# A hybrid convolution, attention and recurrence layer on one core: softmax with a maximum pass for every group and the recurrence in 64 runs per image, in place of softmax without the pass and one recurrence over all images

## The chip, the cores and the metric

The kernel runs on one core of one Trainium2 chip. The metric is the device time of one execution in microseconds (us). Before the change the median of three runs is 23558.29 us (23557.13 to 23570.37). Engines are named as in the profile: PE (matmul) and PEld (its weight loads), DVE (vector), ACT (scalar), POOL, and SP, whose queue issues the DMAs.

## The reference

Everything is float32. The input x has 32 images of 128 channels and 64 x 64 = 4096 places. Layer 0 adds a convolution with a kernel of its own for every image. Layer 1 takes the places as tokens and adds windowed attention (16 wide, 4 heads of 4, windows of 144 tokens at a stride of 72), then a recurrence over the 4096 tokens of each image:

```python
x = x + _L0_conv_ref(_gn(x), L0_conv_kernels, L0_conv_fc_w, L0_conv_fc_b)
t = _to_tokens(x)
t = t + _L1_attn_ref(_ln_t(t),
...
)
t = t + _L1_ffn_ref(_ln_t(t), L1_ffn_W, L1_ffn_V, L1_ffn_gamma, L1_ffn_beta)
x = _from_tokens(t, x)
```

The two parts that the change touches are the softmax of the attention and the recurrence:

```python
scores = jnp.einsum('nhqd,nhkd->nhqk', q, k) / np.float32(np.sqrt(HD))
attn = jax.nn.softmax(scores, axis=-1)
...
Wx = jnp.einsum('bti,hi->bth', x, W)
mean = jnp.mean(flat, axis=0)
var = jnp.var(flat, axis=0)
Wx = ((flat - mean) * jax.lax.rsqrt(var + BN_EPS) * gamma + beta).reshape(B, T, H)
def step(yt, wx_t):
    yt = jax.nn.sigmoid(wx_t + yt @ Vt)
    return (yt, yt)
_, ys = jax.lax.scan(step, y0, jnp.swapaxes(Wx, 0, 1))
```

The mean and the variance run over all tokens of all images, so the recurrence can begin only when the last image has its W z. V is the orthogonal factor of a QR decomposition.

## The kernel before, in words

Line numbers are those of the profile. Channels lie on the 128 partitions, the places of an image along the free dimension, in blocks of 512.

*Stage one, the images* (`images`, L240). A loop over 32 images (L592) calls `front` of the next image, then `attention` and `tail` of the current one. A scheduler orders the instructions of each engine by their dependencies, pools of buffers limit how far it runs ahead. `front` (L295) loads x, normalises it by groups, mixes the convolution kernel (L343 to L346), runs the convolution as nine products per block (L354), and normalises by token: `norm` (L272) with products at L278 and L282, `spread` (L290) that lays the token's factor over all channels. `attention` (L411) projects to 16 (L419), transposes (L431), and works in eight groups of seven windows (the last of six). A group has q and k by L450, v by L470, and then for each window and each pair of heads a set of four score products (L496), one exponential over the set (L504), and four products with v (L510). A column of ones in v gives the sum of each row, by which L529 and L531 divide between two rounds of transposes (L525, L536). L552 leads back to 128 channels. The tiles `sc` for scores have two buffers in PSUM.

`tail` (L568) normalises again, adds to x, stores the sum x2 (L575), normalises once more to z, multiplies a block by W only for its mean and variance (L585, L586), and stores z (L587), both in chunks of 128 places, so that the second stage reads them as [chunk, channel, image, place].

*The branch.* L195 to L236 work out a bound on the scores from the weights and load it to a register. At L599 the kernel takes `images(False)` where the bound is small enough, otherwise `images(True)`, which differs by `shift` (L374): it forms the scores a first time with q and k exchanged (L383), takes each row's largest by DVE (L390), transposes the negated maxima (L401), and adds them to a fifth row of q, whose partner in k is one (L409).

*Stage two, the recurrence* (L605 to L667). From the mean and variance come a scale and a shift; the scale is folded into W (L621 to L625). For each of 4096 places one product with V over 32 images (L661) adds to W z, which L638 wrote into PSUM for 16 places at a time, and one sigmoid (L665) writes y. Per 128 places DVE adds y to x2 (L666) and the sum is stored (L667). Loads of the next chunk run ahead (L629).

Of the kernel before, what the change touches and what calls it, by code (L numbers as in the profile page):

```python
# [10 lines left out]
ALU = mybir.AluOpType  # L11
# [18 lines left out]
SUB = 16  # L30


@with_exitstack
def hybrid_kernel(
# [34 lines left out]
    x2_d = dram.tile([NCH, P, NB, CH], F32, name="x2_d")  # L69
    z_d = dram.tile([NCH, P, NB, CH], F32, name="z_d")  # L70
# [122 lines left out]


    bdr = const.tile([P, DK], F32, name="bdr")  # L195
    nc.sync.dma_start(bdr, b_down.partition_broadcast(P))
    ipr = const.tile([P, 3 * DK], F32, name="ipr")
    nc.sync.dma_start(ipr, in_proj_b.partition_broadcast(P))
    ipT = const.tile([DK, 3 * DK], F32, name="ipT")
    nc.sync.dma_start(ipT, in_projT)  # L200
    okf = const.tile([P, 1], F32, name="okf")
    oki = const.tile([P, 1], mybir.dt.int32, name="oki")
    with tc.tile_pool(name="sb1", bufs=1) as sb1, tc.tile_pool(
        name="ps1", bufs=1, space=bass.MemoryType.PSUM
    ) as ps1:
        one_ = sb1.tile([P, P], F32, name="one_")
        nc.vector.memset(one_, 1.0)
        w2 = sb1.tile([P, DK], F32, name="w2")
        nc.vector.tensor_mul(w2, wd[:, 0:DK], wd[:, 0:DK])
        n_ps = ps1.tile([P, 3 * DK], F32, name="n_ps")  # L210
        nc.tensor.matmul(n_ps[:, 0:DK], one_, w2, start=True, stop=True)
        xm = sb1.tile([P, DK], F32, name="xm")
        nc.scalar.activation(xm, n_ps[:, 0:DK], AF.Sqrt, scale=1.02 * P)
        nc.scalar.activation(bdr, bdr, AF.Abs)
        nc.vector.tensor_add(xm, xm, bdr)
        xmax = sb1.tile([P, 1], F32, name="xmax")
        nc.vector.tensor_reduce(xmax, xm, axis=AX.X, op=ALU.max)
        nc.scalar.activation(ipT, ipT, AF.Abs)
        nc.scalar.activation(ipr, ipr, AF.Abs)
        r_ps = ps1.tile([P, 3 * DK], F32, name="r_ps")  # L220
        nc.tensor.matmul(r_ps, one_[:DK, :], ipT, start=True, stop=True)
        qk = sb1.tile([P, 3 * DK], F32, name="qk")
        nc.vector.scalar_tensor_tensor(qk, r_ps, xmax, ipr, ALU.mult, ALU.add)
        pr_ = sb1.tile([P, NH, HD], F32, name="pr_")
        nc.vector.tensor_mul(
            pr_.rearrange("p h f -> p (h f)"), qk[:, 0:DK], qk[:, DK : 2 * DK]
        )
        sm = sb1.tile([P, NH], F32, name="sm")
        nc.vector.tensor_reduce(sm, pr_, axis=AX.X, op=ALU.add)
        smx = sb1.tile([P, 1], F32, name="smx")  # L230
        nc.vector.tensor_reduce(smx, sm, axis=AX.X, op=ALU.max)
        nc.vector.tensor_scalar(okf, smx, 60.0 / HD**-0.5, None, ALU.is_le)
        nc.vector.tensor_copy(oki, okf)

    bnst = const.tile([P, NB * NBLK, 6], F32, name="bnst")
    small = nc.values_load(oki[0:1, 0:1], min_val=0, max_val=1)  # L236
# [3 lines left out]
    def images(shifted):  # L240
        with ExitStack() as pa:
            keep = pa.enter_context(tc.tile_pool(name="keep", bufs=1))
            big = pa.enter_context(tc.tile_pool(name="big", bufs=2))
            one = pa.enter_context(tc.tile_pool(name="one", bufs=1))
            wrk = pa.enter_context(tc.tile_pool(name="wrk", bufs=2))
            sml = pa.enter_context(tc.tile_pool(name="sml", bufs=3))
            p_sc = pa.enter_context(tc.tile_pool(name="p_sc", bufs=2, space=bass.MemoryType.PSUM))
            p_mm = pa.enter_context(tc.tile_pool(name="p_mm", bufs=2, space=bass.MemoryType.PSUM))
            p_av = pa.enter_context(tc.tile_pool(name="p_av", bufs=2, space=bass.MemoryType.PSUM))

            gx = keep.tile([P, H + 2, W + 2], F32, name="gx")
            nc.gpsimd.memset(gx, 0.0)
            nr = HD + 1 if shifted else HD
            if shifted:
                mx = keep.tile([HALF, NWG, 2, P], F32, name="mx")
                nc.gpsimd.memset(mx, 0.0)
            vas = []
            for i in range(2):
                va = keep.tile([HALF, 2 * NWG, NH, 32], F32, name=f"va{i}")
                nc.gpsimd.memset(va, 1.0)  # L260
                vas.append(va)

            def mm_tile():
                return p_mm.tile([P, BLK], F32, name="mm")

            def sc_tile():
                return p_sc.tile([P, 2, BLK], F32, name="sc")

            def av_tile():
                return p_av.tile([P, BLK], F32, name="av")  # L270

            def norm(src, dst):  # L272

                var = av_tile()
                for i in range(NBLK):
                    s = slice(i * BLK, (i + 1) * BLK)
                    ps = mm_tile()
                    nc.tensor.matmul(ps, cen, src[:, s], start=True, stop=True)  # L278
                    sq = wrk.tile([P, BLK], F32, name="sq")
                    nc.scalar.activation(sq, ps, AF.Square)  # L280
                    nc.scalar.copy(dst[:, s], ps)
                    nc.tensor.matmul(  # L282
                        var, avg[:, P - i : 2 * P - i], sq, start=(i == 0), stop=(i == NBLK - 1)
                    )
                rs = wrk.tile([P, BLK], F32, name="rs")
                nc.scalar.activation(rs, var, AF.Sqrt, bias=eps)
                nc.vector.reciprocal(rs, rs)  # L287
                return rs

            def spread(rs, i):  # L290
                ps = mm_tile()
                nc.tensor.matmul(ps, row[:, i, :], rs, start=True, stop=True)  # L292
                return ps

            def front(b):  # L295
                xt = big.tile([P, T], F32, name="xt")
                for i in range(4):
                    s = slice(i * (T // 4), (i + 1) * (T // 4))
                    nc.sync.dma_start(xt[:, s], xf[b, :, s])


                st = sml.tile([P, NBLK, 6], F32, name="st")
                for i in range(NBLK):
                    nc.vector.bn_stats(st[:, i, :], xt[:, i * BLK : (i + 1) * BLK])
                mv = sml.tile([P, 2], F32, name="mv")
                nc.vector.bn_aggr(mv, st.rearrange("p i s -> p (i s)"))
                gm_ps = mm_tile()
                nc.tensor.matmul(gm_ps[:, 0:1], grp, mv[:, 0:1], start=True, stop=True)
                gm = sml.tile([P, 1], F32, name="gm")
                nc.vector.tensor_copy(gm, gm_ps[:, 0:1])  # L310
                dev = sml.tile([P, 1], F32, name="dev")
                nc.vector.tensor_sub(dev, mv[:, 0:1], gm)
                cv = sml.tile([P, 1], F32, name="cv")
                nc.vector.scalar_tensor_tensor(cv, dev, dev, mv[:, 1:2], ALU.mult, ALU.add)
                gv_ps = mm_tile()
                nc.tensor.matmul(gv_ps[:, 0:1], grp, cv, start=True, stop=True)
                gr = sml.tile([P, 1], F32, name="gr")
                nc.scalar.activation(gr, gv_ps[:, 0:1], AF.Sqrt, bias=eps)
                nc.vector.reciprocal(gr, gr)
                nc.vector.tensor_scalar(  # L320
                    gx[:, 1 : H + 1, 1 : W + 1],
                    xt.rearrange("p (h w) -> p h w", w=W),
                    gm,
                    gr,
                    ALU.subtract,
                    ALU.mult,
                )


                pl = sml.tile([P, P], F32, name="pl", bufs=1)  # L330
                nc.vector.tensor_scalar_mul(pl, dev.to_broadcast([P, P]), gr)
                lg_ps = mm_tile()
                nc.tensor.matmul(lg_ps[:, 0:NK], pl, fcwT, start=True, stop=True)
                co = sml.tile([P, NK], F32, name="co")
                nc.vector.tensor_add(co, lg_ps[:, 0:NK], fcb)
                nc.scalar.activation(co, co, AF.Tanh, scale=0.5)
                nc.scalar.activation(co, co, AF.Exp, scale=0.5)
                cs = sml.tile([P, 1], F32, name="cs")
                nc.vector.tensor_reduce(cs, co, axis=AX.X, op=ALU.add)
                nc.vector.reciprocal(cs, cs)  # L340
                nc.vector.tensor_scalar_mul(co, co, cs)
# [380 lines left out]
```

## Time and profile before

| what | value |
|---|---|
| median of three runs | 23558.29 us |
| the profiled execution | 23570.37 us |
| its span, first to last instruction | 23568.3 us |
| mean granted PE clock | 0.606 |
| PE busy | 19439.3 us (82%) |
| PEld busy | 10946.6 us (46%) |
| DVE busy | 2800.0 us (12%) |
| ACT busy | 5923.9 us (25%) |
| POOL busy | 10.7 us |

A matmul in float32 stands in the profile as two records, each with its weight load, so 14,080 score products are 28,160 records at L496. The end of a matmul's record is modelled, and records of products in different parts of the array overlap; the mean of a record is therefore longer than the pitch at which such products follow each other. The dearest groups of instructions, busy time and mean, and the idle time before them:

```profile
L510 PE MATMUL av<-ex,va 72*32 72x144 f32 x28160 | 4142.7, 448 | 1151.4 <-ACT ex L504 1151.4
L496 PE MATMUL sc<-qs,ks 4*72 4x144 f32 x28160 | 3970.3, 466 | 0.0
L661 PE MATMUL wx<-yk,fVT 128*128 128x32 f32 x8190 | 2557.4, 406 | 1449.4 <-ACT yk L665 1449.4
L504 ACT ACTIVATE ex<-sc 72x576 f32<-72x576 f32 x3520 | 2220.5, 645 | 5865.4 <-PE sc L496 5864.7
```

The first number after the bar is the time in which at least one instruction of the group was running, the second the mean length of one in ns, the third the idle time of its engine just before, with what ended it.

### The profile page before, as it was taken

The page shows a single profiled execution, that of the slowest core. Times are in us where ns is not written, and L with a number is a line of the kernel's source. Part 1 is how long each engine was busy: PE and PEld are TensorE (multiplying, and loading weights), DVE is VectorE, ACT ScalarE, POOL GpSimd, SP SyncE. Part 2 cuts the span into 40 slices and gives each one's busy share as a digit, 9 for nine tenths or more (in the row PEclk, how much of TensorE's full clock was granted, in tenths as well). Part 3 has the DMA queues.
Part 4 walks back from the last instruction along what each step waited for, and adds up shares of the span by engine and source line. Part 5 has one row for each costly group of instructions (what it writes and reads, how often), then busy time and mean ns, then how long its engine had stood idle before and what let it go on. Part 6 is the DMA issues. An engine that isn't in the chain of part 4 may idle for free.

```text
span 23568.3 us, 200944 instructions
## 1 busy us (share of the span) xinstructions
PE 19439.3 (82%) x90183; PEld 10946.6 (46%) x90183; DVE 2800.0 (12%) x3848; ACT 5923.9 (25%) x11369; POOL 10.7 (0%) x41
## 2 busy tenths in 40 slices
PE   8888888888888888888888888888888876666666
PEld 4444444444444444444444444444444444444444
DVE  1111111111111111111111111111111010000000
ACT  2222222222222222222222222222222222222222
POOL 0000000000000000000000000000000000000000
PEclk7666666666666666666666666666666555555555
DMA  0000000000000000000000000000000011111111
GB/s 12 11 11 11 11 11 11 11 11 11 11 11 11 11 11 11 11 11 11 11 11 11 11 11 11 11 11 11 11 11 11 8 43 43 47 46 47 43 47 36
DMA packets 427366, 418.25 MB, mean 18 GB/s; under 512 B 8176, under 2 KB 401792, under 8 KB 418176
## 3 DMA queue, kind: packets, MB, share of 16 engines
q1 hardware_dynamic: 426496, 405.32, 5.4%
q8 instruction: 709, 11.62, 0.2%
q14 instruction: 161, 1.32, 0.0%
HBM read 203.97 MB, written 201.33 MB: 17 GB/s over the span
## 4 chain that ended last, share of the span: by engine, by line
PE 76%; ACT 15%; DVE 6%; issue 3%; ACTq 0%; DMA 0%; SPq 0%
PE av L510 17%; PE wx L661 11%; PE sc L496 11%; PE mm L354 9%; ACT ex L504 8%; PE sc L450 6%; ACT yk L665 5%; PE mm L470 3%; PE mm L278 3%; PE mm L292 3%; PE av L282 3%; PE sc L525 2%; PE wx L638 2%; PE sc L536 2%; PE mm L552 2%
## 5 line engine op out<-in xcount | busy, mean ns | idle before, releaser
L510 PE MATMUL av<-ex,va 72*32 72x144 f32 x28160 | 4142.7, 448 | 1151.4 <-ACT ex L504 1151.4
L496 PE MATMUL sc<-qs,ks 4*72 4x144 f32 x28160 | 3970.3, 466 | 0.0
L661 PE MATMUL wx<-yk,fVT 128*128 128x32 f32 x8190 | 2557.4, 406 | 1449.4 <-ACT yk L665 1449.4
L504 ACT ACTIVATE ex<-sc 72x576 f32<-72x576 f32 x3520 | 2220.5, 645 | 5865.4 <-PE sc L496 5864.7
L510 PEld LDWEIGHTS av<-ex,va 72*32 72x32 f32 x28160 | 2027.0, 159 | 2989.1 <-ACT ex L504 2472.7
L496 PEld LDWEIGHTS sc<-qs,ks 4*72 4x72 f32 x28160 | 2535.1, 222 | 1317.6 <-issue 1281.8
L661 PEld LDWEIGHTS wx<-yk,fVT 128*128 128x128 f32 x8190 | 2086.3, 311 | 2239.3 <-ACT yk L665 2103.0
L354 PE MATMUL mm<-gx,wb 128*128 128x512 f32 x4608 | 2035.0, 604 | 214.5 <-DVE wb L345 214.5
L665 ACT ACTIVATE yk<-wx,shf 128x32 f32<-128x32 f32 x4096 | 1175.7, 287 | 3257.1 <-PE wx L661 3257.1
L354 PEld LDWEIGHTS mm<-gx,wb 128*128 128x128 f32 x4608 | 888.6, 194 | 1337.2 <-issue 1337.2
L292 PE MATMUL mm<-rs,row 128*128 128x512 f32 x1536 | 968.8, 758 | 468.2 <-DVE rs L287 436.7
L280 ACT ACTIVATE sq<-mm 128x512 f32<-128x512 f32 x768 | 464.9, 605 | 3443.2 <-PE mm L278 3443.1
L529 DVE RECIPROCAL rd<-sc 126x32 f32<-126x32 f32 (+1 forms) x256 | 91.6, 358 | 9347.1 <-PE sc L525 9347.1
L470 PEld LDWEIGHTS mm<-wv,gt 32*72 32x72 f32 x7040 | 905.3, 235 | 284.3 <-issue 170.9
L450 PE MATMUL sc<-gt,wq 32*128 32x504 f32 x1024 | 896.6, 1023 | 100.8 <-DVE gt L431 100.8
L552 PE MATMUL mm<-oc,wc 20*128 20x504 f32 (+1 forms) x1024 | 932.7, 1062 | 30.6 <-ACT oc L542 30.6
L450 PE MATMUL sc<-gt,wk 32*128 32x504 f32 x1024 | 906.9, 1037 | 0.0
L470 PE MATMUL mm<-wv,gt 32*72 32x16 f32 x7040 | 872.8, 274 | 0.0
L292 PEld LDWEIGHTS mm<-rs,row 128*128 128x128 f32 x1536 | 334.4, 236 | 1045.4 <-DVE rs L287 516.1
L282 PE MATMUL av<-sq,avg 128*128 128x512 f32 x1536 | 802.4, 641 | 0.5 <-ACT sq L280 0.5
L666 DVE TENSOR_TENSOR xk<-xk,yk 128x4096 f32<-128x4096 f32 x32 | 238.3, 7447 | 4208.8 <-ACT yk L665 4208.8
L455 ACT ACTIVATE qs<-sc,bq 128x504 f32<-128x504 f32 x512 | 531.8, 1141 | 737.0 <-PE sc L450 737.0
(133 smaller groups left out, 9371.2 us busy)
## 6 DMA issues: line engine op xcount, KB each, us to landing
xt<-in_x_dram SPq DMA_DIRECT2D x128, 512.0 KB, 5.6
x_d<-xt SPq DMA_DIRECT2D x32, 2048.0 KB, 9.3
z_d<-zt SPq DMA_DIRECT2D x32, 2048.0 KB, 9.3
zk<-z_d SPq DMA_DIRECT2D x32, 2048.0 KB, 7.6
xk<-x_d SPq DMA_DIRECT2D x32, 2048.0 KB, 7.8
out_dram<-xk SPq DMA_DIRECT2D x32, 2048.0 KB, 9.2
kT<-in_conv_k_dram SPq DMA_DIRECT2D x1, 2304.0 KB
wq<-in_in_projT_dram SPq DMA_DIRECT2D x8, 1.0 KB, 1.7
```

The source lines that it names most:

```text
L278: nc.tensor.matmul(ps, cen, src[:, s], start=True, stop=True)
L282: nc.tensor.matmul(var, avg[:, P - i : 2 * P - i], sq, start=(i == 0), stop=(i == NBLK - 1))
L292: nc.tensor.matmul(ps, row[:, i, :], rs, start=True, stop=True)
L354: nc.tensor.matmul(ps, wb[:, t, :], gx[:, 8 * i + di : 8 * i + di + 8, dj : dj + W], start=(t == 0), stop=(t == 8),)
L450: nc.tensor.matmul(ps[:, c, 0:GH], wt[rows, u, :], gf[rows, c, :], start=True, stop=True)
L470: nc.tensor.matmul(vp[:HALF, o : o + DK], gf[rows, c, HALF * m : HALF * (m + 1)], wv[rows, u, :], start=True, stop=True,)
L496: nc.tensor.matmul(ps[:HALF, j, c * WIN : (c + 1) * WIN], ks[hr : hr + nr, c, HALF * m : HALF * (m + 1)], qs[hr : hr + nr, o : o + WIN], s ...
L504: nc.scalar.activation(ex, ps[:HALF, :, 0 : 2 * WIN], AF.Exp, scale=HD**-0.5)
L510: nc.tensor.matmul(ap[32 * h : 32 * h + 32, (m - m0) * WIN : (m - m0 + 1) * WIN], va[:, 2 * m + c, h, :], ex[:, j, c * WIN : (c + 1) * WIN ...
L552: nc.tensor.matmul(ps[:, 0 : 4 * n], wc, oc[:, 4 * n * i : 4 * n * (i + 1)], start=True, stop=True,)
L661: nc.tensor.matmul(ps[:, t, :], fVT, prev, start=False, stop=True, skip_group_check=True)
L665: nc.scalar.activation(prev, ps[:, t, :], AF.Sigmoid, bias=shf)
```

## The change

The test on the weights' bound and the second copy of the image stage go; what `shift` did stands in `attention` for every group, with the fifth row of q and k always in use. In `tail`, W z is copied from PSUM over z by ACT and stored in place of z; x2 and W z are stored as one row of 4096 places per channel and image. Scale and shift are applied later, to W z. A new test takes the row sums of the absolute values of V times its transpose, and where the largest is at most 1.2 the recurrence is done by runs, otherwise by steps as before (with the scale as a diagonal matrix in the place of W).

By runs, the 4096 places of an image are 64 runs of 64. Every run begins 32 places early, from a plain sigmoid of the first of them, and its first 32 results are dropped; the first run of an image begins at zero. So one step works on the same place of 64 runs of two images, 128 columns: one product with V, one multiply-add on DVE, one sigmoid on ACT, which writes y over W z. There are 16 pairs of images, three of them in flight in three streams; after a pair POOL adds y to x2.

```diff
-    x2_d = dram.tile([NCH, P, NB, CH], F32, name="x2_d")
-    z_d = dram.tile([NCH, P, NB, CH], F32, name="z_d")
+    x2_d = dram.tile([NB, P, T], F32, name="x2_d")
+    z_d = dram.tile([NB, P, T], F32, name="z_d")
...
-        nc.vector.tensor_scalar(okf, smx, 60.0 / HD**-0.5, None, ALU.is_le)
...
+        nc.tensor.matmul(vv, fVT, fVT, start=True, stop=True)
+        nc.scalar.activation(va_, vv, AF.Abs)
+        nc.vector.tensor_reduce(vr, va_, axis=AX.X, op=ALU.add)
+        nc.tensor.transpose(vt_, vr.to_broadcast([P, P]), ident)
+        nc.vector.tensor_reduce(vm, vt_, axis=AX.X, op=ALU.max)
+        nc.vector.tensor_scalar(vm, vm, 1.2, None, ALU.is_le)
...
-                    if shifted:
-                        shift(qs, ks, nw)
+                for m in range(nw):
+                    o = m * WIN
+                    for pr in range(2):
+                        ps = sc_tile()
...
-                                            ks[hr : hr + nr, c, HALF * m : HALF * (m + 1)],
-                                            qs[hr : hr + nr, o : o + WIN],
+                                        ks[hr : hr + HD + 1, c, HALF * m : HALF * (m + 1)],
+                                        qs[hr : hr + HD + 1, o : o + WIN],
...
                 nc.vector.bn_stats(bnst[:, b * NBLK + i, :], wp)
+                nc.scalar.copy(zt[:, s], wp)
...
+            def load(g):
+                if g < NG:
+                    zs[g] = zp.tile([P, NI, NRUN, RUN], F32, name="zr")
+                    for i in range(NI):
+                        nc.sync.dma_start(
+                            zs[g][:, i].rearrange("p c r -> p (c r)"), z_d[g * NI + i]
+                        )
+            for g in range(NSTR + 1):
+                load(g)
+            def stream(j):
...
+                for g in range(j, NG, NSTR):
+                    zt = zs[g]
+                    for r in range(RUN - WARM, RUN):
+                        y, z = yw[r % 2][:, :, 1:], zt[:, :, 0 : NRUN - 1, r]
+                        if r == RUN - WARM:
+                            nc.scalar.activation(y, z, AF.Sigmoid, bias=shf, scale=scl)
+                        else:
...
+                    prev = yw[(RUN - 1) % 2]
+                    for r in range(RUN):
+                        h = hp.tile([P, NI, NRUN], F32, name=f"h{j}")
+                        ps = p_v.tile([P, NI, NRUN], F32, name=f"v{j}")
+                        nc.tensor.matmul(ps, fVT, prev, start=True, stop=True)
+                        nc.vector.scalar_tensor_tensor(
+                            h, zt[:, :, :, r], scl, ps, ALU.mult, ALU.add
+                        )
+                        prev = zt[:, :, :, r]
+                        nc.scalar.activation(prev, h, AF.Sigmoid, bias=shf)
+                        yield
+                    for i in range(NI):
+                        xk = xp.tile([P, T], F32, name="xr")
+                        nc.sync.dma_start(xk, x2_d[g * NI + i])
+                        nc.gpsimd.tensor_add(xk, xk, zt[:, i].rearrange("p c r -> p (c r)"))
+                        nc.sync.dma_start(of[:, g * NI + i], xk)
+                    load(g + NSTR + 1)
...
+    with tc.If(contr > 0) as arm:
+        by_runs()
     with arm.Else():
-        images(True)
+        by_steps()
```

Sizes: RUN = 64, WARM = 32, NI = 2 images to a pair, NSTR = 3 streams, NSTR + 1 = 4 buffers for W z.

## Prediction

> **What bounds the kernel now.** I read the page first: its slices and its chain of waits, for where the time is and at what TensorE clock; then busy time by stage; then the chain inside one attention group and inside the recurrence. The page's slices show two stages, the images (slices 1 to 32) and the recurrence (the last eight, where DMA and a flat 5 in PEclk appear):
>
> ```profile
> PE   8888888888888888888888888888888876666666
> ...
> PEclk7666666666666666666666666666666555555555
> DMA  0000000000000000000000000000000011111111
> ...
> PE 76%; ACT 15%; DVE 6%; issue 3%; ACTq 0%; DMA 0%; SPq 0%
> ```
>
> Busy time by stage gives the border (columns: length, then busy us and count of PE, PEld, DVE, ACT, POOL, then clock, DMA share, GB/s). The first two rows are the attention and the rest of one image:
>
> ```profile
> 5023.00:5429.00 406.00, 360.93 (x2205) 214.42 (x2204) 20.11 (x42) 115.05 (x168) 0.00 (x0) 0.50 0.00 1
> 5429.00:5620.00 191.00, 154.61 (x343) 59.40 (x342) 59.67 (x76) 33.10 (x60) 0.10 (x1) 0.89 0.11 33
> 0.00:19094.60 19094.60, 16449.23 (x81476) 8749.74 (x81476) 2552.93 (x3807) 4746.67 (x7271) 10.70 (x41) 0.63 0.04 11
> 19094.60:23568.30 4473.70, 2990.10 (x8707) 2196.81 (x8707) 247.11 (x42) 1177.25 (x4098) 0.00 (x0) 0.50 0.13 46
> ```
>
> Two numbers carry what follows: the recurrence is 4473.7 us in all, and attention runs at half clock. In the recurrence the chain alternates between PE and ACT, one step each 1.02 us, and 4096 steps of it are 4178 us; the rest is the stage's ends and the block products of L638:
>
> ```profile
> 19989.83 0.65 PE wx L661 x2
> 19990.48 0.03 issue
> 19990.51 0.29 ACT yk L665
> 19990.80 0.04 issue
> ```
>
> In attention the timeline at the start of a group shows the prices needed below (start, length):
>
> ```profile
> 5079.03 3.46 PE L470 MATMUL mm<-wv,gt 32*72 32x16 f32 x28
> ...
> 5082.34 1.25 PE L496 MATMUL sc<-qs,ks 4*72 4x144 f32 x14
> 5082.53 0.39 DVE L477 COPY va<-mm 72x224 f32<-72x224 f32 x1 [5.88 <-PE mm L470]
> 5083.68 0.65 ACT L504 ACTIVATE ex<-sc 72x576 f32<-72x576 f32 x1 [3.31 <-PE sc L496]
> 5084.38 0.68 PEld L510 LDWEIGHTS av<-ex,va 72*32 72x32 f32 x8 [1.23 <-ACT ex L504]
> 5084.38 1.18 PE L510 MATMUL av<-ex,va 72*32 72x144 f32 x8 [0.79 <-ACT ex L504]
> ```
>
> A set of four score products, in two row groups, takes 1.24 us (two sets lie here side by side, in four row groups); DVE starts 0.04 us after PE ends (5082.49 to 5082.53); PE starts 0.05 us after ACT ends; from the first score product to the first av product are 2.04 us.
>
> [...]
>
> **The change part by part.**
>
> *1. The shift pass is now run for every group (the test for small scores is gone).* Before, the branch took the arm without it: no DVE reduce to maxima stands in its trace. The changed kernel's instruction order on PE has per group, between the v products and the first score products, 56 products (14 sets of 4), then 14 transposes; nothing else lies between them, so no PE work covers the pass. DVE gets 14 reduces and two adds per group, ACT idles. The score tiles have two buffers, so set i+2 waits until reduce i has read its tile.
> - Reduce, 72x576 from PSUM: [...]0.755 us, an estimate.
> - One buffer's cycle: 1.24 PE + 0.04 + 0.755 DVE + 0.05 = 2.085 us; two buffers, so 1.04 us a set.
> - Reduce 13 of 14 ends at 2.035 + 6 x 2.085 = 14.55 us after the pass starts, which frees the tile for the transposes. Each is 128 stationary columns; L525 (126 to 128 columns, same clock) starts one each 0.213 us. 14 x 0.213 = 2.98, to 17.6. The first add (L371 and L362, the same kind: 0.69) ends at 17.0, beside the transposes; the second beside the first score set.
> - So the first score set starts at 17.6 instead of 0: **17.6 us per group**; in the group of six windows two sets and two transposes less, 15.1. Per image 7 x 17.6 + 15.1 = 138.3; times 32: **+4,430 us**.
> - Bounds: if DVE alone paced it (0.80 a set) 14.7 a group, 3,700 us;[...] I take the middle since two buffers and three known durations give it.
> - Fifth row in the score products: no time, as the pitch is that of columns.
>
> *2. Tail of an image: W z copied back by ACT, then stored.* 256 copies like L281's 0.59 us. The tile is also read by bn_stats (L586, 0.70 us), beside which the copy runs; its buffer is wanted again only after the next spread and multiply, 0.87 + 0.70 us later. Taken at nothing; were the cover gone, 256 x 0.6 = 150 us. The stores are one long row per partition instead of 512-byte pieces; they lay beside the next image and do so still. The row-sum test of V at the start takes the place of the one removed: a few us either way.
>
> *3. Recurrence by runs.* Removed: 4473.7 us. Added: 16 pairs of images x 96 steps = 1536 steps in three streams. Stream 0 has six pairs, 576 steps one after another; PE's order has the three streams taking turns for most of it and stream 0 alone for about the last 70. A step is product, DVE multiply-add, sigmoid:
> - PE, N = 128 at half clock: L661 takes 0.64 us in two passes with N = 32, of 53 ns each at the pitch seen above. With N = 128 a pass is 213 ns; the first lies beside the second weight load as before, the second adds 0.16: 0.80; with the strided operand (L638 runs some 9% over its pitch) 0.84.
> - DVE: L573's form has 0.744 us at 512, so 0.35 at 128; z read at a stride of 256 bytes, and L666, also strided, shows 1.82 instead of 1.04 ns per element: 0.44.
> - ACT: L665 0.287 at 32 and L426's slope of 0.83 ns: 0.37[...]; written with a stride, as L455 against L426 shows (+0.9 ns per element), 0.53.
> - Three handovers 0.13. Step 1.94 us in 64 of 96, 1.78 in the warm-up: 1.89. The three engines' load per round of three steps, 1.3 to 1.6 us, fits below it, so latency sets the round.
> - 576 x 1.89 = 1,090 us. Entry: the last z store 10.3 us (in the chain of before) and two z loads of 7.6. Exit: two POOL adds[...], and a store of 9.2. Sum **1,145 us**.
> - Queues: after a pair, SP holds its x loads, the two stores (which wait for POOL), then the z loads of the pair four later. That z is [...]due a third of a pair later, 32 rounds or 60 us. All transfers, one at a time at 7.6, 7.8 and 9.2 us, are 32 x 24.6 = 787 us, below 1,090. Both are hidden, with little to spare.
> - Bounds: the clock opens[...]: 1.5 a step, 920 us; turns on in-order queues or late z: 1,500 us.
>
> Sum: 23568.3 + 4,430 - 4,473.7 + 1,145 = 24,670; 2 us lie outside the span (23570.4). The median of the three runs is 12 us below this execution, which is nothing here. **24,670 us.**
>
> **Rivals.**
> - *Clock opens in attention (faster).* [...]an iteration of 2.66 us, of which 1.96 is PE, falls to about 1.8: 3,520 x 0.85 = 2,990 us saved, the pass costs about 3,300 (DVE-paced), the runs 920: 20,320. [...]Against it: 406 us closed on end, L450 included[...]. 0.05.
> - *Pass paced by DVE alone:* 23,940. Needs PE sets ready ahead, which two buffers don't allow. 0.06.
> - [...]
> - *Late z or POOL in the runs:* a pair each 85 us instead of 61 adds about 450: 25,120. 0.13.
> - *The branch takes the old loop:* no gain, about 28,000. V comes from a QR, V times its transpose has row sums of 1 against the limit of 1.2: 0.02.
>
> **How the numbers follow.** Forecast 0.64, rivals as given. Range 23,950 to 25,400: it holds the forecast with its bounds on the runs, late z, and part of the DVE-paced case. What a measurement can tell from no change is 0.2%. Faster is the clock's 0.05; 0.01 within 0.2% (DVE-paced and runs at open clock, 23,700 or less); the rest slower.
>
> **What would show it.** Right: images end near 23,520; a reduce of 72x576 of about 0.76 us, x3520, and sets 1.04 us apart; attention at clock 0.50; the last stage near 1,145 us with idle PE waiting for ACT. Wrong: attention above 0.5 in clock, reduces back to back on DVE, a stage after the images over 1,400 us or under 950, DVE or PE waiting for z's DMA.

## The result, and the profile after

The changed kernel takes 24,759.18 us (median of 4 runs, 24,758.39 to 24,764.91) against 23,557.94 us for the kernel before (median of 4 runs): a ratio of 1.0509, with a 95% interval of 1.0491 to 1.0527. It is slower by 1,201 us, and the forecast was 24,670. The profiled execution has a span of 24,763.0 us, 1,194.7 more than before.

The page of the changed kernel, the slices of the span and the chain that ended last:

```profile
PEclk6666556666556666556666555666655666655555
DMA  0000000000000000000000000000000000000034
...
PE 74%; DVE 13%; ACT 11%; issue 3%; ACTq 0%; DMA 0%; SPq 0%; POOLq 0%; DVEq 0%; POOL 0%
```

The recurrence, eight slices before, is now less than two, and its DMA share rises from 1 to 3 and 4 tenths. In the chain DVE goes from 6% to 13% and ACT falls from 15% to 11%: the pass for the maxima has come onto the path, and the sigmoid of 4096 single steps has left it.

Busy time by stage (columns as before: the stretch and its length, then PE, PEld, DVE, ACT, POOL, clock, DMA share, GB/s). The rows are the attention of one image, the rest of that image, all images, and the last stage:

```profile
4683.30:5229.10 545.80, 481.43 (x3194) 309.08 (x3194) 109.98 (x168) 114.28 (x167) 0.00 (x0) 0.50 0.00 1
5229.10:5420.60 191.50, 156.77 (x343) 60.41 (x342) 57.99 (x76) 38.80 (x69) 0.20 (x1) 0.88 0.08 33
0.00:23642.90 23642.90, 20428.30 (x113157) 11826.50 (x113157) 5387.27 (x7835) 4901.97 (x7524) 14.79 (x42) 0.60 0.02 9
23642.90:24763.00 1120.10, 900.62 (x3040) 725.20 (x3040) 652.74 (x1531) 690.59 (x1538) 283.41 (x32) 0.50 0.44 180
```

Set against the rows of before, the whole difference is in three places. Over the 32 images attention grew from a mean of 406.7 to 545.8 us, which is +4,451 us. The rest of an image took 187.4 or 190.4 us before and takes 191.5 now; the mean of 31 differences is 3.1, so +96 us. The last stage is 1,120.1 us in place of 4,473.7, so -3,353.6. The sum is +1,193, and the spans differ by 1,194.7. Attention stays at a clock of 0.50, and DVE, which was busy for 20 us of one image's attention, is now busy for 110. The groups of the page show the work added (score products of the main pass and of the new pass, and the reduces; the idle time after the bar is PE's or DVE's, with what ended it):

```profile
L470 PE MATMUL sc<-qs,ks 5*72 5x144 f32 x28160 | 4068.4, 465 | 215.8 <-DVE qs L457 215.8
L431 PE MATMUL sc<-ks,qs 4*72 4x144 f32 x28160 | 3278.4, 458 | 410.1 <-DVE mx L438 410.1
L438 DVE TENSOR_REDUCE mx<-sc 72x4 f32<-72x576 f32 x3520 | 2502.4, 751 | 1155.8 <-PE sc L431 1155.8
```

The new products are as many as the old (28,160) and nearly as long, the fifth row makes the old ones no longer (466 ns before, 465 now), and DVE sits idle for 1,155.8 us before the reduces, waiting for PE. PE in turn waits 410.1 us for the reduces. Two engines that wait for each other over the same tile may have too few buffers between them, which a run below tests. The timeline of one group, from its first two reduces on, shows the rhythm (start and length in us; the bracket has the idle time before):

```profile
5106.94 1.42 DVE L438 TENSOR_REDUCE mx<-sc 72x4 f32<-72x576 f32 x2 [0.25 <-PE sc L431]
...
5107.75 1.91 PE L431 MATMUL sc<-ks,qs 4*72 4x144 f32 x16 [0.43 <-DVE mx L438]
5109.05 1.42 DVE L438 TENSOR_REDUCE mx<-sc 72x4 f32<-72x576 f32 x2 [0.69 <-PE sc L431]
```

Two reduces run on end (1.42 us), then DVE waits 0.69 us for the next two sets, then the same again: 2.11 us from pair to pair, where the forecast had 2.085.

In the last stage the groups are (columns as in the page):

```profile
L630 PE MATMUL v<-zr,fVT 128*128 128x128 f32 x2016 | 665.8, 469 | 156.1 <-ACT zr L635 113.9
L635 ACT ACTIVATE zr<-h,shf 128x128 f32<-128x128 f32 x1024 | 517.4, 511 | 349.3 <-DVE h L631 346.5
L631 DVE SCALAR_TENSOR_TENSOR h<-zr,scl,v 128x128 f32<-128x128 f32 x1024 | 439.6, 429 | 386.6 <-PE v L630 352.1
...
L640 POOL TENSOR_TENSOR xr<-xr,zr 128x4096 f32<-128x4096 f32 x32 | 283.4, 8878 | 2196.1 <-ACT zr L635 2150.5 <-DMA xr<-x_d 45.6
```

Each engine waits for the one before it in the step: PE for ACT, ACT for DVE, DVE for PE. None of the three is full, so with three streams it should be the length of a step that counts; a run with two streams tests that. POOL hardly waits for a transfer (45.6 us in all).

### The profile page after: what moved, and what is told of

It reads as the page before. It is cut to its first block, busy times and chain, and to the rows that moved or that the text cites. A ratio compares the mean times of both kernels' runs of the same rounds, so it can differ in the third digit from the quotient of the medians.

```text
span 24763.0 us, 256852 instructions
## 1 busy us (share of the span) xinstructions
PE 21328.9 (86%) x116197; PEld 12551.7 (51%) x116197; DVE 6040.0 (24%) x9365; ACT 5592.6 (23%) x9062; POOL 298.2 (1%) x74
## 4 chain that ended last, share of the span: by engine, by line
PE 74%; DVE 13%; ACT 11%; issue 3%; ACTq 0%; DMA 0%; SPq 0%; POOLq 0%; DVEq 0%; POOL 0%
PE av L484 17%; PE sc L470 10%; PE sc L431 9%; PE mm L332 8%; ACT ex L478 8%; PE sc L391 6%; DVE mx L438 5%; PE mm L411 3%; PE mm L270 3%; PE mm L256 3%; PE av L260 3%; PE sc L499 2%; PE sc L449 2%; PE sc L510 2%; PE v L630 2%
## 5 line engine op out<-in xcount | busy, mean ns | idle before, releaser
L484 PE MATMUL av<-ex,va 72*32 72x144 f32 x28160 | 4143.5, 448 | 1021.1 <-ACT ex L478 1018.7
L470 PE MATMUL sc<-qs,ks 5*72 5x144 f32 x28160 | 4068.4, 465 | 215.8 <-DVE qs L457 215.8
L431 PE MATMUL sc<-ks,qs 4*72 4x144 f32 x28160 | 3278.4, 458 | 410.1 <-DVE mx L438 410.1
L470 PEld LDWEIGHTS sc<-qs,ks 5*72 5x72 f32 x28160 | 2626.9, 222 | 1588.7 <-issue 1313.6
L431 PEld LDWEIGHTS sc<-ks,qs 4*72 4x72 f32 x28160 | 2506.6, 226 | 1073.2 <-DVE mx L438 1073.1
L438 DVE TENSOR_REDUCE mx<-sc 72x4 f32<-72x576 f32 x3520 | 2502.4, 751 | 1155.8 <-PE sc L431 1155.8
L630 PE MATMUL v<-zr,fVT 128*128 128x128 f32 x2016 | 665.8, 469 | 156.1 <-ACT zr L635 113.9
```

The lines of the kernel that those rows point to most:

```text
L431: nc.tensor.matmul(ps[:HALF, j, c * WIN : (c + 1) * WIN], qs[hr : hr + HD, o + HALF * c : o + HALF * (c + 1)], ks[hr : hr + HD, :, HALF * ...
L438: nc.vector.tensor_reduce(mx[:, m, :, 64 * pr : 64 * pr + 64].rearrange("p c (j f) -> p j c f", f=32)[:, :, :, HD], ps[:HALF, :, 0 : 2 * W ...
L470: nc.tensor.matmul(ps[:HALF, j, c * WIN : (c + 1) * WIN], ks[hr : hr + HD + 1, c, HALF * m : HALF * (m + 1)], qs[hr : hr + HD + 1, o : o + ...
L484: nc.tensor.matmul(ap[32 * h : 32 * h + 32, (m - m0) * WIN : (m - m0 + 1) * WIN], va[:, 2 * m + c, h, :], ex[:, j, c * WIN : (c + 1) * WIN ...
L630: nc.tensor.matmul(ps, fVT, prev, start=True, stop=True)
```

## The experiments

Ten runs, in three batches on chips that ran the kernel before in the same batch (medians 23,542 to 23,558 us). Where a kernel computes less than the layer, its text says what it leaves out.

**The gain alone.** The images of before with their branch, and the recurrence by runs.

```diff
+    with tc.If(small > 0) as arm:
+        images(False)
+    with arm.Else():
+        images(True)
...
     with tc.If(contr > 0) as arm:
         by_runs()
```

> The images of before, with its test and its arm without the maximum pass, and the recurrence by runs of the changed kernel (W z copied back and stored). Theory, two independent parts that only add: 19,095 for the images and 1,126 for the runs, with 0 to 110 us for the copy: 20,220 to 20,330 us, a ratio of 0.858 to 0.863 to before; the last stage 1,110 to 1,140 us. Rival, the runs are only as fast as the trace after shows because of the images stage in front of them (clock, layout): above 20,500.[...]

Measured: 20,294.2 us (20,291.22 to 20,295.98), ratio 0.8616 (0.8602 to 0.8631), as expected. Its last stage:

```profile
19169.10:20289.40 1120.30, 899.81 (x3040) 723.89 (x3040) 652.88 (x1531) 690.38 (x1538) 283.32 (x32) 0.50 0.44 180
```

The last stage is the same 1,120 us as in the changed kernel. So the change is two edits that don't touch each other: the runs are worth -3,264 us (20,294 against 23,558), and doing the pass for every group costs 4,465 (24,759 against 20,294). This kernel beats both. Its images have the copy of W z and the new rows, but not the pass, and take 593.7 us in the mean from one to the next in place of 591.7 before, some 60 us in all.

**The cost alone.** The changed images with the old loop: the limit of the new test is set so that the branch takes the steps.

```diff
-        nc.vector.tensor_scalar(vm, vm, 1.2, None, ALU.is_le)
+        nc.vector.tensor_scalar(vm, vm, 0.5, None, ALU.is_le)
```

> The changed kernel with the limit of the row sums of V set to 0.5, so that the recurrence goes by steps. Theory, additive parts: 23,640 for the images and 4,470 for the steps: 28,110 us, within 60. Rival, the steps suffer from the new layout of x2 and z in rows of 4096 (their loads pick 512-byte pieces): some hundred us more, with the steps waiting for DMA.

Measured: 28,081 us, one run, as expected; the last stage takes 4,468 us, so the steps do not suffer from the new rows. The rival in which the branch takes the old loop was put at 28,000; the changed kernel doesn't do so.

**What paces the pass: a shorter reduce.** The reduce reads half of each row of scores, so the shift is the largest of half the keys only.

```diff
-                            ps[:HALF, :, 0 : 2 * WIN].rearrange("p j (c k) -> p j c k", c=2),
+                            ps[:HALF, :, 0 : 2 * WIN].rearrange("p j (c k) -> p j c k", c=2)[:, :, :, 0:HALF],
```

> The changed kernel with the maxima taken over the first half of each window's keys only (the other half of the maximum is left out), so that a reduce reads 288 elements instead of 576. Theory, two score tiles in turn, each cycle 1.24 PE + handovers + reduce: the reduce falls from 0.75 to 0.45 us and two sets take 1.79 instead of 2.09 us: 2.1 us less per group, 440 to 550 us in all: 24,210 to 24,330. Rival, DVE paces the pass: 0.3 less for each set, 4.2 us a group, 1,070 us: 23,690. Rival, PE paces it: no change, 24,760.

Measured: 24,167.8 us, one run, 42 us below the range expected. The reduces' group in its page:

```profile
L438 DVE TENSOR_REDUCE mx<-sc 72x4 f32<-72x288 f32 x3520 | 1504.9, 453 | 1557.4 <-PE sc L431 1557.3
```

A reduce shortened by 298 ns (751 to 453) shortens the pair's cycle by as much, from 2.11 to 1.81 us, and DVE idles more (1,557.4 us in place of 1,155.8). That is a loop through PE, DVE and one buffer. If DVE alone had set the pace, a set would have shortened by 0.30; it did by 0.15. From the first reduce of a full group to its last are 11.27 us in place of 13.34. Attention as a whole is 544 us shorter, as expected. A further 57 us lie in the other part of the images, which this edit does not touch; the part on the copy comes back to them.

**What paces the pass: a third score tile.** Every third set of the pass takes the space of the two tiles for the products with v, which become one larger buffer.

```diff
-        p_av = pa.enter_context(tc.tile_pool(name="p_av", bufs=2, space=bass.MemoryType.PSUM))
+        p_av = pa.enter_context(tc.tile_pool(name="p_av", bufs=1, space=bass.MemoryType.PSUM))
...
-                        ps = sc_tile()
+                        ps = av2_tile() if (2 * m + pr) % 3 == 2 else sc_tile()
```

> The changed kernel with a third score tile in the maximum pass, made of the two buffers of the av products (which then have one buffer). Theory, two tiles set the pace of the pass: reduces now follow each other at 0.76 to 0.82 us instead of 1.05, the pass falls by 2.5 to 3.3 us per group; the av products wait for their copy once or twice per group, 0.6 to 0.8 us each, so 250 to 650 us less in all: 24,110 to 24,510. Rival, PE sets the pace: reduces stay 1.0 us or more apart and the whole is slower than 24,760 by the new waits.

Measured: 23,620 us, one run, 1,139 below the changed kernel and 490 below the range expected. The reduces in its trace (minimum, median and maximum in ns), and the idle time before them:

```profile
L441 DVE TENSOR_REDUCE mx<-sc x2496: 744/751/757, 272.3 to 22369.8; 72x4 f32<-72x576 f32 x192
L441 DVE TENSOR_REDUCE mx<-av x1024: 743/746/748, 273.6 to 22370.4; 72x4 f32<-72x576 f32 x171
...
  PE sc L434: 119.8, 256
```

The reduces are as long as before, but DVE now waits for PE once per group (256 times, 119.8 us) and otherwise goes from one to the next. First to last takes 9.12 us per full group in place of 13.34. Attention as a whole is 1,082 us shorter; again 62 us more lie in the rest of the images, although there the products into the tiles `av` now have one buffer less. The waits of the v products that were feared do not show: PE is idle before them for 1,021.5 us in all, and for 1,021.1 in the changed kernel. So two buffers were what held the pass, and with three it is DVE. Its pace is 0.70 us a set, less than the 0.80 that I had taken for a DVE without pauses.

**The copy of W z.** The copy in `tail` is left out; z is stored, so the recurrence reads z in the place of W z.

```diff
                 nc.vector.bn_stats(bnst[:, b * NBLK + i, :], wp)
-                nc.scalar.copy(zt[:, s], wp)
```

> The changed kernel without the copy of W z back by ACT in the tail (z is stored in its place, so the recurrence reads z and not W z). Outside attention an image takes 191.5 us after the change and 187.4 or 190.4 us before. Theory, the copy adds some 0.5 us to the last block and the start of the convolution, and [...]it falls by one window, to 733.9 us: 24,650. Rival, copy without effect: 737.3 us per image and 24,760 as before. Rival, the copy alone costs: a period that is not a multiple, 736.5 to 737: 24,740.

Measured: 24,664.9 us (24,661.19 to 24,672.75), ratio 1.0469 (1.0452 to 1.0487), 94 below the changed kernel and near the 24,650 expected. A window in these expectations is a step of 3.413 us: in the traces before and after, successive changes of the granted clock lie whole multiples of it apart. The theory takes the time from image to image for a whole number of such steps, 215 of which are 733.9 us. But here the images take anything from 733.6 to 736.2 us from one to the next. And the kernel with the pass and the old loop has the copy too, and nine of its images were as short as here (733.9 us from image to image, in place of 737.3). So the two were run once more, side by side:

> The changed kernel once more, unaltered, beside the one without the copy. Clock-window theory: [...]the profile shows either 737.3 (216 windows) or 733.9 us (215) per image, and both kernels of this pair take the same number or can swap it; the time lies within 24,650 to 24,765 us. Rival, the copy costs one window per image: this kernel at 24,750 to 24,765 again and the one without the copy 90 to 100 us below it.

> The changed kernel without the copy of W z in the tail of the images (z is stored and the recurrence reads z in the place of W z, so its values are not the layer's). Clock-window theory: within 30 us of the unaltered kernel of this pair when both take the same number of windows, 100 us off in either direction when not. Copy theory: 24,655 to 24,675 us, 90 to 100 below the unaltered kernel of this pair.

Measured: with the copy 24,749.24 us (24,744.03 to 24,759.96), ratio 1.0512 (1.0494 to 1.0529); without it 24,665.02 (24,661.05 to 24,669.04), ratio 1.0476 (1.0459 to 1.0494). The difference is 84 us, just under the 90 to 100 of the copy theory. The other theory, in which the run and not the copy settles how many windows an image takes, allowed 100 us where the two take different numbers, and they do: 28 of 31 images with the copy take 737.2 or 737.3 us, none without it over 736.2. So this pair alone doesn't refute it. But over both pairs eight executions with the copy took 24,744 us or more, and eight without it 24,673 or less. In this kernel the copy does cost some 84 to 94 us. Part of it shows in the timeline of `tail`, first with the copy, then without (both at full clock):

```profile
8239.09 0.70 DVE L557 BATCH_NORM_STATS2 bnst<-mm 128x6 f32<-128x512 f32 x1 [1.28 <-PE mm L556]
8239.82 0.59 ACT L558 COPY zt<-mm 128x512 f32<-128x512 f32 x1 [3.09 <-DVE bnst L557]
...
8240.78 1.10 PE L556 MATMUL mm<-zt,fWT 128*128 128x512 f32 x2 [0.87 <-DVE zt L554]
...
8241.91 0.70 DVE L557 BATCH_NORM_STATS2 bnst<-mm 128x6 f32<-128x512 f32 x1 [1.28 <-PE mm L556]
```

```profile
8213.93 0.70 DVE L557 BATCH_NORM_STATS2 bnst<-mm 128x6 f32<-128x512 f32 x1 [1.22 <-PE mm L556]
...
8215.53 1.12 PE L556 MATMUL mm<-zt,fWT 128*128 128x512 f32 x2 [0.78 <-DVE zt L554]
...
8216.69 0.70 DVE L557 BATCH_NORM_STATS2 bnst<-mm 128x6 f32<-128x512 f32 x1 [1.22 <-PE mm L556]
```

The copy starts only when bn_stats has ended (8239.79 to 8239.82), not beside it, and so do all 256 copies. A block takes 2.82 us with the copy and 2.76 without, as PE waits 0.87 instead of 0.78 us for DVE's product. Seven such steps are 0.4 us of an image, 13 us of all images.

The larger part is elsewhere. The first two blocks of the image shown run at half clock with the copy (4.6 and 3.7 us from one bn_stats to the next) and only one without (3.6). With the copy 30 of the 32 images have two such blocks, without it 14. In the mean over the images the eight blocks take 22.37 in place of 21.03 us, and the whole image 733.7 in place of 730.8; 1.1 us of what is left of the difference lie in attention. These traces agree with a small delay that shifts the moment at which the clock rises from 0.50 to 1.00; what sets that moment was not shown.

The copy doesn't settle this moment alone. With the copy in place, 22 images of the kernel with the old loop have two blocks at half clock, 11 of the one with the short reduce, 5 of the one with the third tile and 2 of the one with the branch kept; in the kernel before, without the copy, 12 have. That the 57 and 62 us above are of this kind too is an estimate from these counts, not shown. So 84 to 94 us are what the copy costs in this kernel, and not a price that holds elsewhere.

**How many streams: two.** The images of before, and two streams.

```diff
-NSTR = 3
+NSTR = 2
```

> The images of the kernel before, with the recurrence in runs and two streams in flight in place of three. Latency theory of the prediction (the chain of one step takes 1.86 us and nothing else binds): 48 steps of the first stream alone and 8 pairs of 96 steps after, 816 steps of 1.86 = 1,518, entry and exit of some 55: a last stage of 1,570 us and a total of 20,744 (20,720 to 20,790). Rival, an engine or the transfers set the pace of 0.62 us per step: the stage stays within 1,130 us and the total at 20,290 to 20,310.

Measured: 20,661.8 us, one run, below the range expected; last stage 1,486 us. A stretch of it:

```profile
19593.00:19653.00 60.00, 42.50 (x130) 30.65 (x130) 27.55 (x65) 28.66 (x66) 11.14 (x2) 0.50 0.51 210
```

65 steps of DVE in 60 us make a round of two steps 1.85 us, as long as a round of three (1.86), so the latency theory holds and the rival, 0.62 us a step whatever the number of streams, falls. The stage is 84 us shorter than expected, since the second stream starts 16 us after the first and not after 48 steps.

**How many streams: four.** The images of before and four streams. To make room, the convolution's table is given back before the recurrence, and x2 is added in quarters.

```diff
-NSTR = 3
+NSTR = 4
...
+                        for q in range(4):
+                            s = slice(q * (T // 4), (q + 1) * (T // 4))
+                            xk = xp.tile([P, T // 4], F32, name="xr")
```

> The images of before with their branch, the recurrence by runs with four streams instead of three (x2 added in quarters of an image, the convolution weights' buffer given back before). Theory, latency of a step sets the round of three: with four streams 384 steps one after another at 1.93 us, or 2.05 if ACT at 0.51 us a step is now full: 800 to 860 us for the last stage instead of 1,126, 19,900 to 20,030 us in all. Rival, three streams are at an engine's bound already: a round of four takes 2.5 us or more, the stage stays at 1,050 to 1,150. Rival, transfers bound it: 200 MB at the rate of before take 787 us, and the stage shows waits of DVE or PE for DMA.

Measured: 20,216.5 us (20,215.33 to 20,220.4), ratio 0.8582 (0.8568 to 0.8596): the fastest version here that computes the whole layer, but far behind what was expected. The last stage of 1,061 us is as long as the rival with an engine's bound has it, but the round of 2.5 us that this rival needs isn't there. Two stretches of it:

```profile
19240.00:19360.00 120.00, 118.33 (x536) 83.68 (x536) 109.69 (x269) 112.81 (x270) 18.33 (x8) 0.99 0.12 44
19500.00:19980.00 480.00, 449.03 (x1475) 350.00 (x1473) 315.78 (x738) 332.01 (x745) 149.66 (x64) 0.50 0.58 208
```

Early on 269 steps of DVE in 120 us are 0.45 us a step, at a clock of 0.99. In the second stretch, with all streams past their first pair, a step takes 0.65 us at a clock of 0.50, and the steps recur three to a round of 1.86 us: only three streams are in flight, as in the changed kernel. A z tile is handed back late. After the first add of the first pair at 19335.6 the last of its eight adds ends at 19360.4, with pauses for x2, and only then the next z load leaves; for the second pair the same takes from 19376.6 to 19408.0, because its loads of x2 stand behind that z load.

After the first pairs, however, the tile is no longer what the fourth stream waits for. This shows when the steps of each stream are followed through the trace. The z tile of the tenth pair had landed at 19554.7, the stream that takes it ended its earlier pair at 19562.1, and began the tenth only at 19637.6, 75 us later. What keeps it away there is its place in the engines' order of instructions, in which three streams take turns. To see whether the late hand-back is behind this order, it was taken out.

**Four streams without the addition.** The tile of a pair is stored as it is; x2 is neither loaded nor added.

```diff
-                            nc.sync.dma_start(xk, x2_d[g * NI + i, :, s])
-                            nc.gpsimd.tensor_add(
-                                xk, xk, zt[:, i].rearrange("p c r -> p (c r)")[:, s]
-                            )
-                            nc.sync.dma_start(of[:, g * NI + i, s], xk)
+                        nc.sync.dma_start(
+                            of[:, g * NI + i], zt[:, i].rearrange("p c r -> p (c r)")
+                        )
```

> Four streams in flight as in the run with four, but the addition of x2 is left out: the pair's tile goes straight from the recurrence to the output, with no load of x2 and no POOL work. Hand-back theory (the fourth stream waits for a z tile that is freed only after the x2 load, the POOL additions and the next z load, some 50 us against a lag of 42): the last stage falls from 1,061 to about 456 rounds of 1.8 us plus 60 = 880 us, total 20,030 (19,990 to 20,090). Rival, the written order of the streams or an engine holds the pace: the stage stays above 1,020 us, total above 20,170.

Measured: 19,985.9 us, one run, and the last stage takes 840 us, somewhat less than the 880 expected; the rival, over 1,020 us, falls. A long stretch of it:

```profile
19500.00:19800.00 300.00, 291.53 (x1360) 218.67 (x1360) 266.39 (x680) 273.58 (x688) 0.00 (x0) 1.00 0.48 198
```

680 steps in 300 us are 0.44 us a step, four to a round of 1.76, at full clock throughout this stretch. So the engines can carry four streams, and without the hand-back all four are in the order. The likely reading is that the scheduler, which makes this order beforehand, leaves the fourth stream out where it expects the tile late. That isn't shown: the run takes out the addition, its loads and POOL's work at once, and no run kept them under another order.

## Why the prediction was right, point by point

*The pass, +4,430 us: measured +4,451.* The mechanism held, two buffers that PE and DVE hand to each other. The reduce was put at 0.755 us and takes 0.751, and 288 elements fewer take 298 ns less (751 to 453), 1.03 ns an element. Two other DVE operations that read PSUM, in the trace before, lead to the same 0.755:

```profile
L362 DVE TENSOR_TENSOR xt<-xt,mm 128x512 f32<-128x512 f32 x256 | 176.0, 688 | 1886.9 <-PE mm L354 1886.9
L477 DVE COPY va<-mm 72x224 f32<-72x224 f32 x224 | 86.8, 387 | 1224.4 <-PE mm L470 1224.4
```

From 224 to 512 elements is 301 ns, 1.045 ns an element, and 64 elements more than 512 make 755 ns. That a reduce would keep this rate was an estimate; at twice the time an element, which the forecast put at 25,870 us in all with a probability of 0.10, it would have taken 1.36 us. The cycle of a buffer was 2.085 us and is 2.11, though the sets are not evenly 1.04 us apart: their reduces start 0.675 and 1.436 us apart in turn. The run with the short reduce and the one with the third tile confirm the mechanism from both sides.

From the start of the pass to the first product with v pass 19.61 us, where 2.04 + 17.6 = 19.64 were forecast, against 2.06 measured in the same way before. That it fits so closely is luck in part, since two errors cancel. The end of the same group shows them:

```profile
5120.41 1.94 PE L449 MATMUL sc<-ident,mx 72*128 72x72 f32 x14 [0.20 <-DVE mx L438]
5122.47 1.27 DVE L457 TENSOR_TENSOR qs<-qs,sc 128x504 f32<-128x504 f32 x2 [1.44 <-PE sc L449]
5123.20 1.88 PE L470 MATMUL sc<-qs,ks 5*72 5x144 f32 x14 [0.84 <-DVE qs L457]
```

The fourteen transposes take 1.94 us and not 2.98: these write 72 columns each and start 0.120 us apart, while the 0.213 us of the forecast is that of L525, with 128 columns each. And the first add does not run beside them but after them, so that PE waits 0.84 us for it, 215.8 us over all groups.

*The bound on that term was wrong.* "DVE alone" at 0.80 us a set was to be 3,700 us. With three tiles DVE does run alone, and at 0.70 us a set; attention is 1,082 us shorter than with two, which leaves 3,369 us for the pass. The step that failed is the handover of 0.04 added to the whole length of a reduce: two reduces that find their tiles ready start 0.675 us apart, less than one lasts.

*The tail's copy, taken at nothing: 84 to 94 us.* This is the mis-sized term. The three parts miss by +21 (pass), +96 (rest of the images) and -25 us (recurrence), which is the 89 us between forecast and median within 3. The step that failed is "beside which the copy runs": the copy follows bn_stats, and each block then takes 0.06 us longer, 13 us in all. The larger part came with the clock, which rises later in an image (two blocks at half clock in 30 of 32 images, against 14 without the copy); that a delay of this size could go with that was not thought of. How much of the +96 is this depends on the length of attention too, since 57 and 62 us of it went away with the copy in place. The stated cost without cover, 150 us, bounds it.

*The recurrence, 1,145 us: measured 1,120.* The estimates of its parts were 0.44 us for DVE (0.429), 0.53 for ACT (0.511) and 0.41 for ACT in the warm-up (0.400). The trace before has no add on POOL, so the forecast's time for it rested on no trace; one of 128x4096 takes 8.88 us. A step of a stream comes to 1.86 us where 1.89 was forecast. From the first multiply-add to the last are 1,078 us where 1,090 were forecast, and entry and exit take 42 us where 55 were. The 1,078 hold something that was not forecast: followed through the trace, the first stream takes 171 to 175 us for a pair, and from its third pair on 10.7 us pass before the next one begins. The shorter step and these pauses nearly cancel.

That hand-back and loads are hidden "with little to spare" was right for three streams except at the first change of pairs: the two stretches of 60 us after the first pair ends hold 75 and 66 steps of DVE instead of 98, about 33 us of waiting, and after that a stretch holds 93 to 98.

*Rivals.* The clock did not rise in attention (0.50 throughout). One argument for this, L450 in the 406 us at half clock, was misread: its eight products keep PE full from 5021.24 to 5026.50, and until 5023.13 the clock was still at 1.00. Another stretch of the trace before carries the argument better, 13.5 us in which PE is never idle and the clock stays at half:

```profile
5068.80:5082.30 13.50, 13.50 (x41) 7.26 (x41) 1.67 (x3) 4.16 (x4) 0.00 (x0) 0.50 0.01 1
```

In the runs the clock stayed at 0.50 too, but for 3.4 us. With four streams in flight it was 1.00 (the 300 us above), and the stage took 840 us, so the bound of 920 us named for a full clock was within reach.

## What to carry to other kernels

Price a pass by the loop that goes through the buffer: producer, handover, consumer, handover, divided by the number of buffers, and compare it with each engine alone (here 2.11 / 2 us against 0.70 for DVE, and a third tile was worth 1,139 us). Before parallel streams are added, trace how long a buffer is away after its last use, its add and its reload included. When they are added, look in the trace at the order in which the engines take their steps: of four streams three were in flight (0.65 us a step), though the engines could carry four (0.44). Don't take a small copy on an idle engine for free where it follows another engine's work: the delay of 0.06 us per block was small, but with it the clock rose later in more images (30 of 32 against 14), and the kernel lost 84 to 94 us.

## What the runs showed of the hardware that was not expected

The records of successive reduces of 72x576 from PSUM overlap: in the changed kernel each lasts 0.751 us, and the two of a pair start 0.675 us apart.

With three streams the clock was 0.50 (PE busy for 900.6 of 1,120.1 us); with four in flight it was 1.00 (PE busy for 291.53 of 300 us), and a round took 1.76 us for four steps, against 1.86 for three. How busy PE is in the profile doesn't by itself tell which: in the run with four streams this stretch, where three were in flight, stayed at 0.50:

```profile
19634.00:19694.00 60.00, 59.33 (x190) 45.18 (x190) 40.38 (x94) 42.70 (x96) 15.60 (x7) 0.50 0.57 208
```

In the traces before and after, each of the 320 gaps between successive changes of the granted clock is a whole multiple of 3.413 us (within 0.002 us, with 3.41333 for the step). In some runs the time from image to image is such a multiple too: 593.8 to 594.1 or 597.2 to 597.4 us before (174 or 175 steps), 737.2 or 737.3 in the changed kernel (216), and nearly all images of the one with the old loop (733.9 or 737.3, 215 or 216). In others it isn't: 733.6 to 736.2 without the copy, 699.9 to 703.3 with the third tile. Why some keep to it was not shown: no run moved the moment at which the clock changes on purpose.
